# An inverse DFT as half sum and half difference on four row groups of TensorE, with one pool of eight PSUM banks

## Chip, core and metric

The kernel runs on one core of a Trainium2 chip. The metric is the device time in microseconds of one execution. Everything is float32.

## What is computed

The input is x of shape (32, 32, 128, 128): 32 images of 32 channels, each a 128 x 128 matrix. Two residual layers follow each other.

```python
# layer 0: group norm, then 5 Newton-Schulz steps for the matrix square root
for _ in range(NUM_ITER):
    T = 0.5 * (3.0 * I - jnp.matmul(Z, Y))
    Y = jnp.matmul(Y, T)
    Z = jnp.matmul(T, Z)
...
x = x + _L0_conv_ref(_gn(x))
# layer 1: group norm, then a spectral convolution on low modes
x_dht = jnp.fft.fftn(x.astype(jnp.complex64), axes=(2, 3)).real
top = jnp.einsum('bixy,ioxy->boxy', x_dht[:, :, :M1, :M2], weights1)
bot = jnp.einsum('bixy,ioxy->boxy', x_dht[:, :, -M1:, :M2], weights2)
out_dht = out_dht.at[:, :, :M1, :M2].set(top)
out_dht = out_dht.at[:, :, -M1:, :M2].set(bot)
y = jnp.fft.ifftn(out_dht.astype(jnp.complex64), axes=(2, 3)).real
x = x + _L1_conv_ref(_gn(x), weights1, weights2)
```

So of each channel's spectrum 64 row modes (first and last 32) by 32 column modes are kept, mixed over the 32 channels with weights of their own for each mode, and transformed back; only the real part is needed.

## The kernel before, in words

**Newton work.** The 32 images are cut into 256 tasks of four channels each. A task goes through `newton` (with `quartic` twice): ten products (`products`, L250) and three transpositions (`transposed`, L256), each over four 128 x 128 matrices into one PSUM bank, and each followed by an evacuation on DVE (`plus`, L244, with a scalar times PSUM plus a tile) or ACT (`taken`, L236 and L238). Pool makes the operand x (L274) and the sums r (L293, L317), in which `eye` is added. Four tasks run at once in four lanes. One pass of the main loop is a round: every lane makes one step of its generator; a task takes 13 rounds. `prep` computes the group norm of the next image (loads xs, L170; statistics on DVE, L178).

**After a task.** `settle` writes the result to a DRAM buffer mid (L337) and lets Pool make sums and differences of mirrored halves (`fold`, L342); `forward` makes the DFT over one axis, `spectrum` over the other one, with the second group norm, and writes the modes to DRAM (xs<-spec, L449).

**Groups.** The images form three groups of 24, 6 and 2. Once a group's spectra are complete, the queue `prods` gets its mode products (`wide_products` for 24, L492; `small_products` for 6 and for 2, L556), whose results are copied to om by ACT (L499, L569) and written to DRAM (od). The queue `backs` gets one `inverse` for each image of the group, behind a marker that waits for the products.

**Inverse.** `inverse(b)` loads the products twice, on partitions 0 to 63 and 64 to 127 (`load_products`, ob, L589), and the input in pieces of eight channels (`load_input`, yt<-mid, L599, 512 KB each, six buffers). The first stage (L628) transforms the 64 row modes: the channel's products are the stationary operand with 32 columns, and the table (cosines or sines, 128 columns) is streamed. It has 64 matmuls in two blocks, one for each half d. ACT copies the result to gt (L638). The second stage (L646) has, for each d and e, two matmuls with 64 rows and 512 columns, each into a bank. DVE adds the bank to yt in place (L651), and yt is written to the output (`store`, L607), from SP's DMA queue, in the tail from ACT's. In all there are 8 second-stage matmuls and 8 adds of 512 elements per image.

**Banks.** The eight PSUM banks are split: five for the Newton products (`ps_ns`), three for all else (`ps_ax`); only in the tail do the other uses alternate between both.

**Order.** Which instruction comes next on each engine is settled at build time, by a scheduler with priorities from the program order; operations wrapped in `kept` keep their order among themselves. Engines execute their own list in order. The rate at which the queues are stepped is in the main loop:

```python
            if i == 0 or tail:
                step(prods)
            if i == 0 or i == 2 and rounds % 2 or tail:
                step(backs)
```

i is the lane. `tail` holds when no Newton task is left; then both queues are stepped at every lane. At the beginning of the tail the lanes' buffers are freed and the weights for the last products are loaded by 14 DMAs from Pool's queue (wt_late, L746).

Of the kernel before, what the change touches and what calls it, by code (L numbers as in the profile page):

```python
# [24 lines left out]
F32 = mybir.dt.float32  # L25
AF = mybir.ActivationFunctionType
ALU = mybir.AluOpType
AX = mybir.AxisListType
PSUM = bass.MemoryType.PSUM
DRAM = bass.MemoryType.DRAM  # L30

P = 128
B = 32
C = 32
G = 16
LANES = 4
GROUPS = (24, 6, 2)


QA = 3 + 12 ** (1 / 3)  # L40
# [4 lines left out]
NB = 8  # L45
# [7 lines left out]
T_FH = slice(64, 192)  # L53
T_IH = slice(192, 448)
T_IW = slice(448, 576)
T_COLS = 576
# [3 lines left out]
def conv_preact_kernel(  # L60
# [16 lines left out]
    make_identity(nc, ident)  # L77
    eye = const.tile([P, 4, P], F32, name="eye")
    for j in range(4):
        nc.vector.tensor_scalar_mul(eye[:, j, :], ident, EYE)  # L80
    avg_mean = const.tile([P, P], F32, name="avg_mean")
# [27 lines left out]
    sets = phase.enter_context(tc.tile_pool(name="sets", bufs=1))  # L109
    ps_ns = ctx.enter_context(tc.tile_pool(name="ps_ns", bufs=5, space=PSUM))  # L110
    ps_ax = ctx.enter_context(tc.tile_pool(name="ps_ax", bufs=3, space=PSUM))

# [6 lines left out]
    tail = False  # L119
    turn = [0]  # L120

    def bank(pool=None):
        if pool is None:
            pool = ps_ax
            if tail:
                turn[0] += 1
                pool = (ps_ax, ps_ns)[turn[0] % 2]
        return pool.tile([P, 4, P], F32, tag="ps", name="ps")

# [111 lines left out]
    def plus(ps, f, t, tag, bufs=4):  # L241

        s = four(tag, bufs)
        nc.vector.scalar_tensor_tensor(s, ps, f, t, ALU.mult, ALU.add)  # L244
        return s

    def products(lhsT, rhs):
        ps = bank(ps_ns)
        for j in range(4):
            nc.tensor.matmul(ps[:, j, :], lhsT[:, j, :], rhs[:, j, :], start=True, stop=True)  # L250
        return ps

    def transposed(t, pool=None):
        ps = bank(pool)
        for j in range(4):
            nc.tensor.transpose(ps[:, j, :], t[:, j, :], ident)  # L256
        return ps
# [38 lines left out]
    def quartic(m, mb, r):  # L296


        v = plus(products(mb, m), -1 / (QA * QR * QS), m, "v", 3)
        yield  # L300
        w = plus(transposed(v, ps_ns), -QA * QS, r, "w", 3)
        yield
        q = plus(products(v, w), -QA / (16 * QS), eye, "q", 3)
        yield
        return q

    def newton(g, sn, xt, m, mb, r):


        q = yield from quartic(m, mb, r)  # L310
        y = taken(products(q, m), "y")
        yield
        m = taken(products(q, y), "m", 3)
        yield
        mb = taken(transposed(m, ps_ns), "mb", 2, QR * QS)
        r = four("r", 4)
        nc.gpsimd.tensor_tensor(r, mb, eye, ALU.add)  # L317
        yield
        q = yield from quartic(m, mb, r)
        pw, py = products(q, m), products(q, y)  # L320
        w, y = taken(pw, "t", 3), taken(py, "y4", 2)
        yield
        t = plus(products(w, q), -0.5 * EYE / 1.5, eye, "t", 3)
        yield
        ps = products(t, y)
        for j in range(4):
            c = 4 * g + j
            nc.vector.scalar_tensor_tensor(  # L328
                xt[:, j, :], ps[:, j, :], sn[:, c : c + 1], xt[:, j, :], ALU.mult, ALU.add
            )  # L330
        yield
# [17 lines left out]
    def forward(b, q, u):  # L349
# [19 lines left out]
        for i in (1, 0):  # L369
# [5 lines left out]
            )  # L375
        sw = sp.tile([P, 4, P], F32, tag="sw", name="sw", bufs=2)
        nc.scalar.copy(sw, ps)
# [10 lines left out]
    def spectrum(b, u, st):  # L388
# [4 lines left out]
        for s in range(2):  # L393
            for i in range(2):
                for e in range(2):
# [7 lines left out]
                    )  # L403
        z = sp.tile([P, 4, P], F32, tag="z", name="z")
        for i in range(2):
# [29 lines left out]
        ps = transposed(z)  # L435
        spec = sp.tile([P, KK, 4, 8], F32, tag="spec", name=f"spec{b}")
        nc.scalar.activation(
# [18 lines left out]
    def wide_products(i):  # L456
# [26 lines left out]
        for step in range(2 * KK):  # L483
# [3 lines left out]
            if not h:  # L487
                om = modes.tile([P, L * C], F32, tag="om", name=f"om{i}_{kk}", bufs=2)
            pm = bank()
            for t in range(4):  # L490
# [8 lines left out]
            nc.scalar.copy(  # L499
                om.rearrange("p (l t o) -> p t l o", l=4, t=8)[:, 4 * h : 4 * h + 4],  # L500
                pm.rearrange("p t (l o) -> p t l o", l=4),
            )
# [9 lines left out]
    def small_products(i):  # L512
# [35 lines left out]
        for kk in range(KK):  # L548
# [18 lines left out]
            if e:  # L567
                om = modes.tile([P, L * C], F32, tag="om", name=f"om{i}_{k2}", bufs=2)[:, 0:512]
                nc.scalar.copy(om, pm.rearrange("p a x -> p (a x)"))  # L569
                done = k2, om  # L570
                if k2 + len(xks) < KK // 2:
                    load_spectra(k2 + len(xks))
# [6 lines left out]
    def load_products(b):  # L579
        if b < B and b not in obs:  # L580
            g, n = where[b]

            obs[b] = inv.tile([P, 4, 8 * C], F32, tag="ob", name=f"ob{b}", bufs=2)
            if GROUPS[g] <= NB:
                src = od[g][:, :, :, n, :].rearrange("k q l x -> (k q) l x")
            else:
                src = od[g][:, :, n, :].rearrange("k q (l x) -> (k q) l x", l=4)
            for e in range(2):
                kept(nc.sync.dma_start(out=obs[b][64 * e : 64 * e + 64], in_=src))  # L589

    def load_input(b, d):

        if (b, d) in yts:
            return
        yts[b, d] = []
        for e in range(2):
            o = 16 * e + 8 * d
            y = inv.tile([P, 8, P], F32, tag="yt", name=f"yt{b}_{o}", bufs=6)
            kept(nc.sync.dma_start(out=y, in_=mid[b][:, o : o + 8, :]))  # L599
            yts[b, d].append(y)  # L600

    stores = []

    def store(lag):
        while len(stores) > lag:
            b, o, y = stores.pop(0)
            kept((nc.scalar if tail else nc.sync).dma_start(out=out[b, :, o : o + 8, :], in_=y))  # L607

    def inverse(b):

        more = where[b][1] < GROUPS[where[b][0]] - 1
        load_products(b)
        load_input(b, 0)
        yield
        ob = obs[b].rearrange("p l (t o) -> p (l t) o", o=C)
        if more:
            load_products(b + 1)
        for d in range(2):
            store(1)

            pg = [bank() for _ in range(2)]
            for j in range(4):
                for i in range(2):
                    for s in range(2):
                        for e in range(2):
                            col = 64 * i + 32 * s
                            rows = slice(64 * e, 64 * e + 64)
                            nc.tensor.matmul(  # L628
                                pg[e][col : col + 32, j, :],
                                ob[rows, :, 16 * e + 8 * d + 4 * i + j],  # L630
                                tab[rows, T_IH.start + s * P : T_IH.start + (s + 1) * P],
                                start=True,
                                stop=True,
                            )
            gts = []
            for e in range(2):
                gts.append(inv.tile([P, 4, P], F32, tag="gt", name=f"gt{b}_{d}_{e}", bufs=3))
                nc.scalar.copy(gts[e], pg[e])  # L638
            yield
            for e in range(2):  # L640
                store(1)

                py = [bank() for _ in range(2)]
                for i in range(2):
                    rows = slice(64 * i, 64 * i + 64)
                    nc.tensor.matmul(  # L646
                        py[i], tab[rows, T_IW], gts[e][rows], start=True, stop=True
                    )
                for i in range(2):
                    y = yts[b, d][e][:, 4 * i : 4 * i + 4, :]  # L650
                    nc.vector.tensor_add(y, py[i], y)  # L651
                stores.append((b, 16 * e + 8 * d, yts[b, d][e]))
                if not e:
                    if d:
                        if more:
                            load_input(b + 1, 0)
                    else:
                        load_input(b, 1)
                yield
        if not more:  # L660
            store(0)

# [72 lines left out]
    while todo or any(lanes) or posts or specs or prods or backs:  # L735
# [11 lines left out]
        for i in range(LANES):  # L747
# [17 lines left out]
            if i == 0 or tail:  # L765
                step(prods)
            if i == 0 or i == 2 and rounds % 2 or tail:
                step(backs)
# [10 lines left out]
def _table():  # L779
# [11 lines left out]
    t[:, T_FH] = np.tile(half, (2, 1))  # L791
    t[:, T_IH] = np.tile(np.concatenate([np.cos(row).T, np.sin(row).T], 1), (2, 1))
    inv = np.concatenate([np.cos(col).T, -np.sin(col).T], 0) / (P * P)
    t[:, T_IW] = np.tile(inv.reshape(2, 8, 4, P).transpose(0, 2, 1, 3).reshape(64, P), (2, 1))
    return t.astype(np.float32)
# [36 lines left out]
```

## Time and profile before

| what | value |
|---|---|
| time, median of 3 runs | 3305.03 us (3302.87 to 3305.51) |
| the profiled execution | 3304.25 us |
| its span, first to last instruction | 3302.3 us |
| mean granted TensorE clock | 0.986 |
| moved by DMA | 479.64 MB, mean 145 GB/s |
| mode products of the group of 24 | about 2210 to 2400 us |
| last Newton product | 3187.6 us |

The profile is one execution. A line of a group of instructions gives its source line, engine, operation and tiles, the shapes, the count after x, then the busy time in microseconds, the mean of one in nanoseconds, and the idle time of the engine before it with what ended that. A float32 matmul appears as two records on PE (a transposition as one), each with its weight load, so that 256 second-stage matmuls are x512; neighbouring records overlap, and the mean of one is longer than the distance between two. A view by stretches gives, for each stretch of time, the busy time of every engine. The chain of waits follows the last instruction back to what released it.

### The profile page before, as it was taken

What the parts mean: (1) busy time and instruction counts of PE and PEld (TensorE: products, weight loads), DVE (VectorE), ACT (ScalarE), POOL (GpSimd) and SP (SyncE); (2) the same over time, 40 slices, a digit from 0 to 9 for tenths busy, and PEclk for the clock granted to TensorE, in tenths of its full rate; (3) what the DMA queues carried; (4) which work ended last, traced back from release to release, by engine and by line L of the source; (5) the groups of instructions that cost most, each with busy time, mean ns of one, the idle gap of its engine ahead of it and who ended that gap; (6) DMA issues with size and microseconds to landing.
All of it is one profiled execution on the core that took longest, in us unless ns stands there. A gap on an engine that the chain in (4) does not pass through costs nothing.

```text
span 3302.3 us, 82823 instructions
## 1 busy us (share of the span) xinstructions
PE 3180.5 (96%) x33216; PEld 2940.7 (89%) x33216; DVE 2273.3 (69%) x6375; ACT 1388.5 (42%) x2865; POOL 1474.2 (45%) x2077
## 2 busy tenths in 40 slices
PE   6999999999999999999999999999999999999984
PEld 6999999999999999999999999999977777878853
DVE  6777777777777777777777777775566666675551
ACT  3444444444444444444444444444433333433321
POOL 4555555554554545545554555553433333333320
PEclk9999999999999999999999999999999999999996
DMA  3333333333332333333333333326687777777686
GB/s 119 97 103 100 103 100 103 100 98 99 95 93 90 98 102 100 103 100 103 100 97 103 100 100 95 94 91 213 213 260 258 237 231 236 240 255 252 217 286 227
DMA packets 273680, 479.64 MB, mean 145 GB/s; under 512 B 83728, under 2 KB 93968, under 8 KB 273296
## 3 DMA queue, kind: packets, MB, share of 16 engines
q1 hardware_dynamic: 194960, 323.33, 30.9%
q10 hardware_dynamic: 76320, 143.69, 14.1%
q0 software_dynamic: 2016, 7.34, 0.5%
q8 instruction: 261, 4.28, 0.5%
q14 instruction: 123, 1.01, 0.1%
HBM read 319.06 MB, written 155.19 MB: 144 GB/s over the span
## 4 chain that ended last, share of the span: by engine, by line
PE 84%; DMA 8%; DVE 6%; issue 1%; SPq 1%; ACT 0%; DVEq 0%; ACTq 0%
PE ps L250 63%; PE ps L256 11%; DMA xs<-in_xt 5%; PE ps L646 3%; PE ps L628 2%; PE ps L360 1%; DVE xt L328 1%; DVE a_st L178 1%; PE ps L556 1%; PE ps L492 1%; PE ps L397 1%; DMA yt<-mid 1%; DMA out<-yt 1%; DVE q L244 1%; DVE yt L651 1%
## 5 line engine op out<-in xcount | busy, mean ns | idle before, releaser
L342 POOL TENSOR_TENSOR fold<-xt 128x256 f32<-128x256 f32 x512 | 365.2, 732 | 863.6 <-DVE xt L328 762.7
L293 POOL TENSOR_TENSOR r<-b,eye 128x512 f32<-128x512 f32 x256 | 326.5, 1275 | 806.6 <-issue 771.1
L250 PE MATMUL ps<-w,v 128*128 128x128 f32 x4096 | 548.5, 277 | 1.2 <-DVE w L244 1.2
L250 PE MATMUL ps<-y,q 128*128 128x128 f32 x4096 | 543.9, 276 | 0.0
L250 PEld LDWEIGHTS ps<-w,v 128*128 128x128 f32 x4096 | 501.6, 193 | 16.7 <-issue 7.4
L250 PEld LDWEIGHTS ps<-y,q 128*128 128x128 f32 x4096 | 498.8, 192 | 7.7 <-issue 7.6
L236 ACT COPY y<-ps 128x512 f32<-128x512 f32 x512 | 300.3, 587 | 387.8 <-PE ps L250 387.0
L274 POOL TENSOR_SCALAR x<-xt,a_nm,a_sc 128x128 f32<-128x128 f32 x1024 | 449.0, 452 | 21.8 <-DVE a_n L206 20.2
L244 DVE SCALAR_TENSOR_TENSOR w<-ps,r 128x512 f32<-128x512 f32 x512 | 350.0, 686 | 108.8 <-PE ps L256 102.3
L284 ACT ACTIVATE b<-b,a_off,a_scr 128x128 f32<-128x128 f32 x1024 | 422.4, 485 | 1.7 <-DMA b<-in_x 1.6
L244 DVE SCALAR_TENSOR_TENSOR q<-ps,eye 128x512 f32<-128x512 f32 x512 | 349.0, 682 | 56.2 <-PE ps L250 42.0
L178 DVE BATCH_NORM_STATS2 a_st<-xs 128x6 f32<-128x128 f32 x1024 | 228.7, 280 | 189.1 <-DMA xs<-in_xt 188.8
L328 DVE SCALAR_TENSOR_TENSOR xt<-ps,a_t_s,xt 128x128 f32<-128x128 f32 x1024 | 292.4, 342 | 80.5 <-PE ps L250 79.6
L238 ACT ACTIVATE mb<-ps 128x512 f32<-128x512 f32 x256 | 153.0, 598 | 462.5 <-PE ps L256 450.6
L317 POOL TENSOR_TENSOR r<-mb,eye 128x512 f32<-128x512 f32 x256 | 326.0, 1274 | 34.8 <-ACT mb L238 34.5
L256 PE MATMUL ps<-ident,v 128*128 128x128 f32 x2048 | 317.9, 275 | 2.4 <-DVE v L244 2.3
L244 DVE SCALAR_TENSOR_TENSOR v<-ps,m 128x512 f32<-128x512 f32 x256 | 175.7, 686 | 200.9 <-PE ps L250 191.2
L250 PE MATMUL ps<-m,q 128*128 128x128 f32 x2048 | 277.4, 278 | 9.6 <-DVE q L244 9.4
L250 PE MATMUL ps<-x,b 128*128 128x128 f32 x2048 | 276.4, 278 | 5.6 <-POOL x L274 5.6
L250 PE MATMUL ps<-y,t 128*128 128x128 f32 x2048 | 280.3, 280 | 0.4
L236 ACT COPY m<-ps 128x512 f32<-128x512 f32 x256 | 150.0, 586 | 307.7 <-PE ps L250 307.6
L250 PEld LDWEIGHTS ps<-m,q 128*128 128x128 f32 x2048 | 248.9, 192 | 30.2 <-DVE q L244 22.7
(115 smaller groups left out, 5022.8 us busy)
## 6 DMA issues: line engine op xcount, KB each, us to landing
b<-in_x ACTq DMA_DIRECT2D x256, 256.0 KB, 3.0
xt<-in_xt ACTq DMA_DIRECT2D x256, 256.0 KB, 3.3
xs<-in_xt SPq DMA_DIRECT2D x256, 256.0 KB, 3.3
mid<-xt SPq DMA_DIRECT2D x256, 256.0 KB, 2.0
yt<-mid SPq DMA_DIRECT2D x128, 512.0 KB, 6.8
out<-yt SPq DMA_DIRECT2D x110, 512.0 KB, 5.8
ob<-od SPq DMA_DIRECT2D x64, 256.0 KB, 5.3
plain<-in_wk SPq DMA_DIRECT2D x18, 512.0 KB, 4.3
```

The source lines that it names most:

```text
L178: nc.vector.bn_stats(st[:, 4 * i + c, :], tiles[i][:, c, :])
L236: nc.scalar.copy(t, ps)
L238: nc.scalar.mul(t, ps, f)
L244: nc.vector.scalar_tensor_tensor(s, ps, f, t, ALU.mult, ALU.add)
L250: nc.tensor.matmul(ps[:, j, :], lhsT[:, j, :], rhs[:, j, :], start=True, stop=True)
L256: nc.tensor.transpose(ps[:, j, :], t[:, j, :], ident)
L274: nc.gpsimd.tensor_scalar(m[:, j, :], xt[:, j, :], nm[:, c // 2 : c // 2 + 1], sc[:, c : c + 1], ALU.add, ALU.mult,)
L284: nc.scalar.activation(mb[:, j, :], mb[:, j, :], AF.Identity, bias=off[:, c : c + 1], scale=scr[:, c : c + 1],)
L293: nc.gpsimd.tensor_tensor(r, mb, eye, ALU.add)
L317: nc.gpsimd.tensor_tensor(r, mb, eye, ALU.add)
L328: nc.vector.scalar_tensor_tensor(xt[:, j, :], ps[:, j, :], sn[:, c : c + 1], xt[:, j, :], ALU.mult, ALU.add)
L342: nc.gpsimd.tensor_tensor(f[:, :, 64 * half : 64 * half + 64], xt[:, :, 0:64], xt[:, :, 64:128], op)
```

## The change

- The first stage uses the mirror symmetry of the output rows: the table now has the cosines for 64 rows and the sines for 64 rows side by side (128 columns), and the stationary operand is four channels with 32 column modes each (128 columns). It is 8 matmuls with 64 rows for an image instead of 64.
- The second stage treats half an image (16 channels) at once. Each of four row groups of 32 partitions holds four channels. With the cosine table it makes the half sum, with the sine table the half difference, each 4 x 64 columns, into the two halves of a bank; four banks are taken. One row (and its counterpart) goes with the cosine table in a matmul of four columns.
- ACT copies the half differences to a tile d (eight copies of 256 elements per image). DVE adds the half sum to both halves of yt, reading it twice by a broadcast (eight adds of 512 elements, as before). Pool then subtracts and adds d on the two halves of yt, in place (eight operations of 512 elements per image).
- The order of elements in om, od and ob is turned, with the weights reordered on the host; for the groups of 6 and 2 ACT makes a copy of 1024 elements per image (from the tile or to ob).
- `inverse` has five calls instead of eight, and `backs` is stepped at lane 0 in two rounds out of three instead of three times in two rounds; in the tail at every lane, as before. Stores are no longer kept back by one.
- One pool of eight banks serves all. `eye` is one matrix, broadcast over four. sw, z and spec share two buffers; om, d and the first load of the small groups' products share three (`page`).

```diff
-T_IH = slice(192, 448)
-T_IW = slice(448, 576)
+T_IH = slice(192, 320)
+T_IW = slice(320, 576)
...
-    eye = const.tile([P, 4, P], F32, name="eye")
-    for j in range(4):
-        nc.vector.tensor_scalar_mul(eye[:, j, :], ident, EYE)
+    eye1 = const.tile([P, 1, P], F32, name="eye")
+    nc.vector.tensor_scalar_mul(eye1[:, 0, :], ident, EYE)
+    eye = eye1.to_broadcast([P, 4, P])
...
-    ps_ns = ctx.enter_context(tc.tile_pool(name="ps_ns", bufs=5, space=PSUM))
-    ps_ax = ctx.enter_context(tc.tile_pool(name="ps_ax", bufs=3, space=PSUM))
+    ps8 = ctx.enter_context(tc.tile_pool(name="ps8", bufs=8, space=PSUM))
...
+    def page(name):
+        return modes.tile([P, 1024], F32, tag="page", name=name, bufs=3)
+
+    def bank():
+        return ps8.tile([P, 4, P], F32, tag="ps", name="ps")
...
-        sw = sp.tile([P, 4, P], F32, tag="sw", name="sw", bufs=2)
+        sw = sp.tile([P, 4, P], F32, tag="sp", name="sw", bufs=2)
...
             nc.scalar.copy(
-                om.rearrange("p (l t o) -> p t l o", l=4, t=8)[:, 4 * h : 4 * h + 4],
-                pm.rearrange("p t (l o) -> p t l o", l=4),
+                om.rearrange("p (o l) -> p o l", l=L)[:, :, 16 * h : 16 * h + 16],
+                pm.rearrange("p t (l o) -> p o (t l)", l=4),
             )
...
-    def store(lag):
-        while len(stores) > lag:
+    def store():
+        while stores:
...
+        ob = obs[b]
+        if GROUPS[where[b][0]] <= NB:
+            ob = inv.tile([P, 1024], F32, tag="ob", name=f"ob{b}", bufs=2)
+            nc.scalar.copy(
+                ob.rearrange("p (o t l) -> p o t l", t=8, l=4),
+                obs[b].rearrange("p (l t o) -> p o t l", l=4, t=8),
+            )
+        ob = ob.rearrange("p (e j m) -> p e j m", e=2, j=4)
         if more:
             load_products(b + 1)
...
+        pg = [bank() for _ in range(2)]
+        for j in range(4):
             for e in range(2):
-                gts.append(inv.tile([P, 4, P], F32, tag="gt", name=f"gt{b}_{d}_{e}", bufs=3))
-                nc.scalar.copy(gts[e], pg[e])
+                rows = slice(64 * e, 64 * e + 64)
+                nc.tensor.matmul(
+                    pg[e][:, j, :], ob[rows, e, j, :], tab[rows, T_IH], start=True, stop=True
+                )
...
+        for e in range(2):
+            store()
+
+            py = [bank().rearrange("p j x -> p (j x)") for _ in range(4)]
+            py = [p.rearrange("p (s c h) -> p s c h", s=2, h=64) for p in py]
+            cos, sin = (slice(T_IW.start + P * i, T_IW.start + P * i + P) for i in range(2))
+            for s, table, h, g in (
+                (0, cos, slice(0, 64), slice(0, 64)),
+                (1, sin, slice(1, 64), slice(65, 128)),
+                (1, cos, slice(0, 1), slice(64, 65)),
+            ):
+                for i in range(4):
+                    rows = slice(32 * i, 32 * i + 32)
+                    nc.tensor.matmul(
+                        py[i][:, s, :, h],
+                        tab[rows, table],
+                        gts[e][rows, :, g],
+                        start=True,
+                        stop=True,
+                    )
+            d = page(f"d{b}_{e}").rearrange("p (c h) -> p c h", h=64)
+            for i in range(4):
+                nc.scalar.copy(d[:, 4 * i : 4 * i + 4, :], py[i][:, 1])
+            for i in range(4):
+                y = yts[b, e][i // 2][:, 4 * (i % 2) : 4 * (i % 2) + 4, :]
+                y = y.rearrange("p c (s h) -> p c s h", s=2)
+                nc.vector.tensor_tensor(
+                    y, py[i][:, 0, :, None, :].to_broadcast([P, 4, 2, 64]), y, ALU.add
+                )
+            for i in range(2):
+                y, di = yts[b, e][i], d[:, 8 * i : 8 * i + 8, :]
+                for half, op in enumerate((ALU.subtract, ALU.add)):
+                    yh = y[:, :, 64 * half : 64 * half + 64]
+                    nc.gpsimd.tensor_tensor(yh, yh, di, op)
+                stores.append((b, 16 * e + 8 * i, y))
+            if not e:
+                load_input(b, 1)
+            elif more:
+                load_input(b + 1, 0)
             yield
...
-            if i == 0 or i == 2 and rounds % 2 or tail:
+            if i == 0 and rounds % 3 or tail:
                 step(backs)
```

## The prediction

> **What bounds the kernel now.** I read the page's first part, then busy time by stretches, then the groups by tile shape, and last the chain that ended last.
>
> ```profile
> PE 3180.5 (96%) x33216; PEld 2940.7 (89%) x33216; DVE 2273.3 (69%) x6375; ACT 1388.5 (42%) x2865; POOL 1474.2 (45%) x2077
> ```
>
> ```profile
> 1000.00:1500.00 500.00, 497.21 (x4484) 481.68 (x4483) 370.47 (x1070) 225.51 (x472) 255.09 (x360) 1.00 0.32 97
> ...
> 2400.00:3188.00 788.00, 769.33 (x9750) 626.32 (x9750) 508.26 (x1275) 296.66 (x600) 258.52 (x362) 0.98 0.75 243
> 3188.00:3303.00 115.00, 54.43 (x1629) 35.88 (x1610) 25.03 (x55) 16.56 (x31) 14.23 (x19) 0.70 0.73 258
> ...
> 3190.00:3200.00 10.00, 6.78 (x156) 3.46 (x152) 3.85 (x7) 1.67 (x3) 3.69 (x3) 1.00 1.00 329
> 3200.00:3210.00 10.00, 7.87 (x82) 3.82 (x84) 4.09 (x7) 2.80 (x6) 6.21 (x10) 0.66 0.99 333
> ```
>
> The columns of a stretch are length, busy us of PE, PE's weight loads, DVE, ACT and Pool, granted clock, DMA share, GB/s. There are three regimes. Up to about 2400 us TensorE is the bound (497 of 500 us) and DMA is a third used. From 2400 to 3188 the Newton work shares PE with the inverse transforms: PE is idle 18.7 us of 788 and DMA is at 0.75. After the last Newton product at 3188 comes a tail of 115 us in which PE is half idle and DMA full: 329 to 333 GB/s at a share of 1.00 is the ceiling that I use for it.
>
> ```profile
> L646 PE MATMUL ps<-gt,tab 64*128 64x512 f32 x512 | 156.5, 658 | 19.4 <-ACT gt L638 10.0 <-DVE yt L651 9.4
> L628 PE MATMUL ps<-tab,ob 64*32 64x128 f32 x4096 | 86.7, 291 | 10.6 <-DMA ob<-od 6.7 <-DVE yt L651 3.7
> ...
> L651 DVE TENSOR_TENSOR yt<-ps,yt 128x512 f32<-128x512 f32 x256 | 166.7, 684 | 125.4 <-PE ps L646 108.0 <-DMA yt<-mid 15.7 <-PE ps L150 1.0
> ...
> L317 POOL TENSOR_TENSOR r<-mb,eye 128x512 f32<-128x512 f32 x256 | 326.0, 1274 | 34.8 <-ACT mb L238 34.5
> ...
> L406 ACT COPY z<-ps 128x256 f32<-128x256 f32 x64 | 20.7, 375 | 85.8 <-PE ps L397 81.1 <-DVE b_d L154 4.7
> ```
>
> These price the pieces: the two PE stages of the inverse, the add on DVE, a 512-element two-input Pool operation (1274 ns) and a 256-element ACT copy out of PSUM (375 ns). The last pieces of the chain:
>
> ```profile
> 3218.96 14.23 DMA xs<-spec
> ...
> 3234.51 3.65 DMA diag<-xs
> ...
> 3238.36 2.41 PE ps L556 x133
> ...
> 3266.72 0.59 ACT om L569
> ...
> 3280.63 6.66 DMA out<-yt
> ...
> 3287.37 9.63 DMA yt<-mid x2
> ```
>
> The last group's mode products cannot begin before its spectrum has been written and read back (3219 to 3238); they take 28.3 us, and the last two inverses another 35.6 us, up to 3302.3.
>
> **What the Trainium skill says.** "TensorEngine Tiling (Array Packing)", Key Properties: tiles operate independently, and a change of tiling mode drains the array. The trace agrees: the four records of an L646 block, each 512 columns or 0.43 us at the Newton rate of 0.107 us per 128 columns, take 1.06 us and not 1.7, and the block costs about 0.1 us on entering. "TensorE: Matmul & The Clock Gate", Why this matters for your kernels: four K=32 tiles with N=512 gave 3.07 times one; no run here shows four row tiles yet. "SBUF — State Buffer", SBUF: two separate sides: Pool and DVE exclude each other where DVE reads two SBUF inputs; the adds here read one from PSUM, and L651 ran at 684 ns beside a Pool that is 33% busy, so I charge nothing.
>
> **The change, part by part.**
>
> *PE per image.* Before: first stage 64 matmuls in two blocks; in the timeline a block runs 2695.94 to 2697.09 with 0.15 us of switching, 1.3 us; second stage four blocks of 1.06 us plus 0.09 of switching. 2 x 1.3 + 4 x 1.15 = 7.2 us. After: the first stage is 8 matmuls of 128 columns, four on each of two row groups; a 128-column matmul is two records 0.107 to 0.111 us apart, so 4 x 0.22 = 0.88, with switching 1.1 us. The second stage, for each half image, is 256 + 252 + 4 columns on each of four row groups. At two records of 0.213, two of 0.21 and two short ones bounded by their weight load (0.11, the spacing of two loads on the same rows) this is 1.07 us if the groups run side by side, 1.3 with switching; 4.3 if they do not. I take 1.3: 1.1 + 2 x 1.3 = 3.7 us. Saved: 3.5 us an image.
>
> *Where the images stand.* A step of the inverse was taken 1.5 times a round and an image took 8 calls, 5.3 rounds; now it is taken in two rounds of three and needs 5 calls, 7.5 rounds. In the instruction order of PE 28 of the 32 inverses stand before the last Newton matmul; in the changed kernel only 21 do. Seven images move into the tail.
>
> *End of the Newton work.* 3187.6 - 28 x 7.2 + 21 x 3.7 = 3063.7. To this come stalls. Of the 18.7 us idle before I keep all. New: DVE now gets four adds in a row (4 x 0.684 = 2.7 us) while PE has 1.3 us of its own; before two adds (1.4) met 1.15. Each of the adds also waits for ACT's copy of the same bank, and four of the eight banks are held meanwhile. 42 half images at nothing (as the slack of a round covers it) to 1.0 us; I take 0.15, 6 us: 3070. Pool gets 8 x 1.274 = 10.2 us an image. Its old work in an image's time is 258.5 us / 28 images, x 7.5/5.3 = 13 us; 23 us of the (3070 - 2400) / 21 = 32 us of an image are busy. Behind these operations stands r for the next w; it has two rounds (6 us) of slack, so I charge nothing, and 1 us per half (42 us) if that cover is gone.
>
> *Tail up to the last products.* The instruction order has images 21 to 29 after the Newton end, and the write of the last spectrum is queued on SP behind the loads of image 29, which wait for the stores of image 28. So eight images must pass. An image moves 2.1 MB in, 2.1 out and 0.5 of products: 4.7 MB at 330 GB/s is 14.3 us. Pool's own chain for an image is 10.2, plus for each half the second store's issue (0.34, on ACT's queue, ahead of the next copies), and two copies (0.75) with hand-overs of 0.2: 12.8 us, below DMA. 8 x 14.3 = 114; the late weights (14 x 512 KB, 7.3 MB, at the 411 GB/s of 3220 to 3230) 18; six buffers already filled, 3.1 MB, -9: 123 us. The spectrum's write and read back took 19 us under load; the queue is emptier now, 3.4 and 3.7 are medians: I take 10 (7 to 19). Products begin at 3070 + 133 = 3203, against 3238.
>
> *End.* 28.3 for the products as before, to 3231. From the last om copy to the end 35.6 before; added are a copy of 1024 elements on ACT (1.1 to 2.4, twice the 512-element rows at 0.59 and 1.2) and Pool's chain, four halves of 6.4 us behind 13 us of loads and first stage, and a store of 4.5: 43. Span 3231.5 + 0.3 + 43 = 3275.
>
> *At nothing.* One pool of eight banks: PE's order to 2200 us is the same but for a few swaps per image, and PE idles 0.5% there, so nothing to gain; a bank taken at a bad moment could cost up to 0.3% of 2200, 7 us. The broadcast eye, shared sw/z/spec buffers and the other strides of om: same element counts on engines with over a quarter of idle time; u's copy (375 ns for 256 with a stride of 512 bytes in PSUM) shows that the stride costs nothing.
>
> The profiled execution lasted 3304.25, 1.95 more than its span, and the median is 3305.03. 3275 + 2 = 3277 us, 0.8% less.
>
> **Rivals.**
> 1. *The tail is paced by Pool and ACT's queue (slower).* A store on ACT waits for Pool, and the next copies, for which Pool waits, stand behind it; Pool also issues the late weights and waited 15.4 us for them before. For it: DVE, Pool, ACT, store and load follow one another in only six buffers. Against: in 3190 to 3213 two images passed in 24 us with the same buffers. From 7.15 to 8.55 us a half image (20 halves at 1.4 = 28 us) the gain is gone; at 9.3 the time is 3320. Chance 0.22.
> 2. *The Newton stretch stalls* on DVE's or Pool's runs, 0.6 us more per half image: 42 x 0.6 = 25, 3302, no change. For it: Pool goes from a third to over 70% busy in this stretch. Against: each Newton round now meets fewer adds on DVE, 8 in 7.5 rounds instead of 8 in 5.3. 0.16.
> 3. *Better than forecast*: 12.3 us per image, as the last two before, and half of the old stalls gone: 16 + 9 less, and the end 8 less: 3244. 0.12.
> 4. *The row groups do not run side by side*: 42 x 3.0 = 126 us later, about 3400. L646 at two groups speaks against it. 0.04.
>
> **How the numbers follow.** The forecast has 0.46, with a range of its own of 3255 to 3297. What tells from no change is 0.2%, 6.6 us, so 3298 to 3312. Rival 2 is mostly there (0.13, the rest slower). Faster 0.46 + 0.12 = 0.58, same 0.13, slower 0.22 + 0.04 + 0.03 = 0.29. The range 3240 to 3328 leaves out rival 4, a third of rival 1 and small ends of the others.
>
> **What would show it.** Second-stage matmuls starting in fours a few ns apart, blocks near 1.1 us; the last Newton product near 3070; a DMA share near 1.00 from there for some 120 us with halves every 7 us; the first product of the last group near 3203; 43 us after its last copy. Wrong it would be if the Newton end came after 3095, or if DMA sat under 0.8 in the tail with Pool waiting for ACT, or if PE before 2200 us lost more than 1%.

## The result and the profile after

The changed kernel takes 3400.37 us (median, 3399.22 to 3405.13) against 3305.27 us for the kernel before beside it: a ratio of 1.0286, interval 1.0267 to 1.0306. It is slower by 2.9%; the forecast was 3277 us. Its profiled span is 3403.3 us (3302.3 before), so the question is where 101 us came from, and 129 us against the span of 3275 us that the prediction worked out.

The first part of the page of the changed kernel:

```profile
PE 3108.6 (91%) x30656; PEld 2973.8 (87%) x30656; DVE 2320.0 (68%) x6372; ACT 1448.5 (43%) x3065; POOL 1787.0 (53%) x2333
```

TensorE did 72 us less than before, as intended, and stood idle 295 us instead of 122. The view by stretches of the changed kernel (length; busy us of PE, its weight loads, DVE, ACT, Pool; granted clock, DMA share, GB/s) shows where:

```profile
500.00:1000.00 500.00, 491.49 (x4428) 475.88 (x4427) 368.07 (x1047) 224.54 (x467) 252.55 (x358) 1.00 0.31 96
...
2450.00:3000.00 550.00, 492.46 (x4653) 463.12 (x4652) 387.58 (x976) 238.24 (x540) 362.74 (x422) 0.96 0.63 206
...
3265.00:3280.00 15.00, 7.38 (x68) 6.89 (x68) 7.09 (x16) 5.45 (x12) 10.10 (x9) 0.50 0.97 322
...
3350.00:3403.00 53.00, 14.15 (x149) 12.01 (x148) 9.94 (x16) 11.17 (x23) 19.72 (x16) 0.50 0.59 184
```

and the same second stretch of the kernel before:

```profile
2450.00:3000.00 550.00, 535.03 (x6215) 433.32 (x6221) 372.23 (x958) 211.03 (x431) 189.18 (x268) 0.98 0.73 239
```

Three things are to be seen. In the first regime, where no inverse runs, PE now idles 8.5 us of 500 instead of 2.7 (497.34 busy before). In the second it idles 57.5 us of 550 instead of 15, while Pool goes from 189 to 363 us busy. In the tail DMA is near its ceiling at 3265, and far from it in the last 53 us.

The groups by shape of the changed kernel, for the instructions that are new:

```profile
L652 PE MATMUL ps<-gt,tab 32*128 32x256 f32 x512 | 59.6, 509 | 54.0 <-ACT gt L636 48.5 <-DVE yt L665 5.4
...
L665 DVE TENSOR_TENSOR yt<-ps,yt 128x512 f32<-128x512 f32 x256 | 158.9, 682 | 194.7 <-ACT d L661 88.5 <-DMA yt<-mid 55.4 <-POOL yt L672 41.1
...
L661 ACT COPY d<-ps 128x256 f32<-128x256 f32 x256 | 76.9, 385 | 145.2 <-POOL yt L672 61.1 <-PE ps L652 53.5 <-DMA yt<-mid 12.2
...
L672 POOL TENSOR_TENSOR yt<-yt,d 128x512 f32<-128x512 f32 x256 | 317.6, 1273 | 187.6 <-DVE yt L665 140.4 <-issue 41.9 <-DMA plain<-in_wk 5.2
```

Their durations are those of the forecast (682 and 684, 1273 and 1274 ns). What is new stands behind the bar: the copy L661 waits for Pool, Pool for the add L665, the add for the copy.

To find the place of each loss I use three points of the trace in every kernel: A, the start of the first Newton record after four fifths of them (16384 of 20480); the last Newton product; and the end. The stretch lies between the first two and contains the inverses that share PE; the tail follows it. These points are good to about 0.2 us.

| kernel | A | stretch | last Newton product | tail | of it: to the last group's products, they, after them | span |
|---|---|---|---|---|---|---|
| before | 2338.8 | 848.4 | 3187.2 | 115 | 51, 28, 36 | 3302.3 |
| after | 2379.2 | 791.1 | 3170.4 | 233 | 150, 30, 53 | 3403.3 |
| forecast | as before | 118 less | 3070 | 204 | 133, 28, 43 | 3275 |

A comes 40 us late, the stretch saved 57 us and not 118, and the tail is 28 us longer than forecast. The sum is 40 + 61 + 28 = 129.

### The profile page after: what moved, and what is told of

The parts are those of the page before. It is cut to its first block, busy times and chain, and to the rows that moved or that the text cites. A ratio compares the mean times of both kernels' runs of the same rounds, so it can differ in the third digit from the quotient of the medians.

```text
span 3403.3 us, 78408 instructions
## 1 busy us (share of the span) xinstructions
PE 3108.6 (91%) x30656; PEld 2973.8 (87%) x30656; DVE 2320.0 (68%) x6372; ACT 1448.5 (43%) x3065; POOL 1787.0 (53%) x2333
## 5 line engine op out<-in xcount | busy, mean ns | idle before, releaser
L289 POOL TENSOR_TENSOR r<-b,eye 128x512 f32<-128x512 f32 x256 | 326.2, 1274 | 646.2 <-issue 600.0
L672 POOL TENSOR_TENSOR yt<-yt,d 128x512 f32<-128x512 f32 x256 | 317.6, 1273 | 187.6 <-DVE yt L665 140.4
L665 DVE TENSOR_TENSOR yt<-ps,yt 128x512 f32<-128x512 f32 x256 | 158.9, 682 | 194.7 <-ACT d L661 88.5
```

What stands on the lines that cost most here:

```text
L672: nc.gpsimd.tensor_tensor(yh, yh, di, op)
```

## The experiments

Eleven kernels, each timed beside the kernel before. A, stretch, tail and span are from one profile each; median and ratio (to the kernel before) are from all runs. Runs of one kernel differ by up to 20 us (a_yield: 3329.62 to 3349.43), and A of a_nopool lies 5 us behind that of the changed kernel, though its edit acts only behind A. So a difference of some 10 us between two stretches proves little by itself.

| kernel | edit | A | stretch | tail | span | median | ratio, interval |
|---|---|---|---|---|---|---|---|
| b_pool8 | before, one bank pool | 2377.6 | 846.3 | 115 | 3338.5 | 3343.31 | 1.0111, 1.0094 to 1.0128 |
| a_yield | after, a step more in prep | 2331.2 | 780.5 | 230 | 3341.9 | 3337.57 | 1.0094, 1.0065 to 1.0123 |
| a_nopool | after, no L672 | 2384.4 | 759.6 | 208 | 3352.1 | 3350.10 | 1.0121, 1.0101 to 1.0140 |
| a_pace | after, old stepping | 2378.1 | 885.5 | 114 | 3377.7 | 3383.43 | 1.0230, 1.0214 to 1.0246 |
| b_pool8_yield | b_pool8 and the step | 2329.5 | 839.0 | 115 | 3283.6 | 3283.81 | 0.9928, 0.9914 to 0.9941 |
| a_yield_xsact | a_yield, xs from ACT | 2324.2 | 760.7 | 230 | 3315.1 | 3321.15 | 1.0037, 1.0022 to 1.0051 |
| a_yield_halfadds | a_yield, half the adds | 2333.8 | 757.9 | 234 | 3325.9 | 3319.63 | 1.0035, 1.0023 to 1.0048 |
| a_yield_spstore | a_yield, tail stores from SP | 2333.9 | 774.1 | 245 | 3353.5 | 3355.92 | 1.0135, 1.0120 to 1.0150 |
| a_free3 | a_nopool, a_yield_xsact, a_yield_halfadds | 2324.4 | 711.8 | 207 | 3242.8 | 3243.90 | 0.9807, 0.9794 to 0.9821 |
| b_pool8_yield_xsact | b_pool8_yield, xs from ACT | 2320.4 | 846.2 | 115 | 3281.4 | 3283.47 | 0.9924, 0.9910 to 0.9937 |
| a_xsact_pace | a_yield_xsact, old stepping | 2323.7 | 880.3 | 116 | 3320.2 | 3318.80 | 1.0034, 1.0021 to 1.0047 |

**The 40 us before any inverse.** Of the change, the bank pool, the shared buffers and the broadcast eye act there (and, near its end, the order of om). The waits of PE in 500 to 1000 us of the changed kernel begin with a line that the kernel before doesn't have (total us, times, longest):

```profile
PE ps L184 <- DVE a_qs L180: 7.1, 5, 1.4
```

Five images pass in that stretch, and each pays once. At one of these places the timeline of PE in the changed kernel (start, us) has

```profile
1033.28 0.26 PE L146 MATMUL ps<-a_ms,avg_mean 128*128 128x16 f32 x1
1034.97 0.38 PE L184 MATMUL ps<-a_qs,avg_mean 128*128 128x32 f32 x2 [1.43 <-DVE a_qs L180]
```

and that of DVE

```profile
1033.58 0.17 DVE L148 COPY a_nm<-ps 128x16 f32<-128x16 f32 x1 [0.26 <-PE ps L146]
1033.79 0.24 DVE L150 TENSOR_TENSOR a_d<-a_st,a_nm 128x64 f32<-128x64 f32 x1
1034.06 0.23 DVE L153 TENSOR_TENSOR a_d<-a_d 128x64 f32<-128x64 f32 x1
1034.32 0.25 DVE L154 SCALAR_TENSOR_TENSOR a_d<-a_d,a_st 128x64 f32<-128x64 f32 x1
1034.60 0.22 DVE L180 TENSOR_REDUCE a_qs<-a_d 128x32 f32<-128x64 f32 x1
```

The matmul for the mean of the group norm (L146) and the one for its mean square (L184) stand next to each other on PE, and between them lies a chain of five DVE instructions: PE has nothing else in its list and waits, 1.7 us between the two records where neighbours are 0.11 apart. In the instruction list of the kernel before Newton products stand between the two in 30 of 32 images; in the changed kernel in none. About 1.6 us (1.69 less 0.11) for each of the 25 images up to A is 40.

b_pool8 puts only the pool into the kernel before:

```diff
-    ps_ns = ctx.enter_context(tc.tile_pool(name="ps_ns", bufs=5, space=PSUM))
-    ps_ax = ctx.enter_context(tc.tile_pool(name="ps_ax", bufs=3, space=PSUM))
+    ps8 = ctx.enter_context(tc.tile_pool(name="ps8", bufs=8, space=PSUM))
+    ps_ns = ps_ax = ps8
```

> The kernel before with one edit: one pool of eight PSUM banks in place of five and three. In the instruction order of this kernel all 32 pairs of small matmuls of the group norm (mean, then mean square) stand next to each other on PE, as in the changed kernel; with five and three there are Newton matmuls between them in 30 of 32. Theory A (PE, in order, waits at the second matmul for a chain on DVE, about 1.6 us an image): about 33 us are lost by the 15360th Newton record and the time is 3335 to 3350 us. Rival (the loss before 2200 us comes from the broadcast eye or the shared small buffers, the bank pool costs nothing): under 8 us lost there, 3300 to 3312.

A came at 2377.6, 38.8 us late, with nothing of the new inverse in the kernel, the time of 3343.31 lies in the range of theory A, and its waits of PE in 500 to 1000 us begin with the same line, under its own numbers:

```profile
PE ps L188 <- DVE a_qs L184: 7.1, 5, 1.4
```

a_yield leaves the pool and only parts the two matmuls, by one step more of the generator:

```diff
         _, nm, d = moments(st, "a")
+        yield
         q = small.tile([P, C], F32, tag="a_qs", name=f"a_qs{b}")
```

> The changed kernel with one more step boundary in the group norm between the mean and the mean-square matmul, so that Newton matmuls stand between the two again (31 of 32). Theory A: the 33 us up to the 15360th Newton record come back, and some more later; 3355 to 3368 us. Rival (the DVE chain or the other shared buffers cost the time and not the neighbouring of the two matmuls): 3390 to 3403.

A came at 2331.2, 48 us earlier than in the changed kernel and 7.6 earlier than before; the stretch lost another 10.6. The time of 3337.57 is below the range expected, 3355 to 3368, as A comes even earlier than in the kernel before. So the pool costs 40 us by the order that it brings about, and not by a lack of banks. With both edits in the kernel before (b_pool8_yield: the two diffs above)

> The kernel before with one pool of eight banks and the step boundary between the two small matmuls of the group norm. In its order 16 Newton matmuls stand between them in 31 images. The changed kernel with the boundary was 12 us ahead of the kernel before at the 15360th Newton record. If that gain belongs to the bank pool and the boundary alone: 12 us ahead there as well, the rest as before, 3288 to 3296. Rival (the gain came with another part of the change, the broadcast eye or the shared buffers): level with before, 3300 to 3310.

PE is busier than in either kernel; the first regime in b_pool8_yield:

```profile
500.00:1000.00 500.00, 497.89 (x4510) 483.97 (x4509) 372.05 (x1077) 228.86 (x475) 255.31 (x364) 1.00 0.34 101
1000.00:1500.00 500.00, 498.84 (x4522) 485.28 (x4522) 372.70 (x1076) 229.59 (x476) 256.53 (x364) 1.00 0.32 96
```

This version beats both kernels; it is 0.7% under the kernel before. Whether the step alone, with five and three banks, would do as well was not tried.

b_pool8_yield and a_yield differ by the new inverse alone, with its stepping, its buffers and the broadcast eye: A agrees within 2 us, the stretch gains 58.5, the tail loses 115. The rest of the experiments divides these two numbers.

**The stretch: 61 us of the saving missing.** The blocks themselves are cheap. The second stage of a half image in the timeline of PE:

```profile
2714.91 1.06 PE L246 MATMUL ps<-w,v 128*128 128x128 f32 x8
2715.89 1.26 PE L652 MATMUL ps<-gt,tab 32*128 32x256 f32 x24
2717.08 1.16 PE L246 MATMUL ps<-m,q 128*128 128x128 f32 x8
```

From its start to the next product it is 1.19 us. The Newton block ahead of it takes 0.98 where 0.89 is usual, so 0.09 us are lost on entering: together 1.28, where 1.3 was forecast. A first stage takes 1.09 and 0.09, 1.18 in all (1.1). By the forecast's terms 21 x 3.7 are 78 us, the other work of the stretch is 628 (848.4 - 28 x 7.2 - 18.7), and the old idle time 18.7: together 724, and 791 were measured. 67 us are new stalls, where 6 were charged. PE's idle time in the stretch shows most of them: 80 us, and 19 in the kernel before.

The longest waits of PE in 2450 to 3000 us of the changed kernel are all for DVE:

```profile
PE ps L252 <- DVE v L240: 18.0, 9, 4.7
PE ps L184 <- DVE a_qs L180: 11.4, 4, 6.0
PE ps L246 <- DVE t L240: 11.3, 4, 7.6
PE ps L246 <- DVE q L240: 7.5, 8, 1.9
```

One such place in the timeline of the changed kernel:

```profile
2717.57 2.48 DVE L665 TENSOR_TENSOR yt<-ps,yt 128x512 f32<-128x512 f32 x4 [0.88 <-ACT d L661]
...
2718.94 4.95 POOL L672 TENSOR_TENSOR yt<-yt,d 128x512 f32<-128x512 f32 x4 [1.83 <-DVE yt L665]
...
2720.89 0.63 DVE L150 TENSOR_TENSOR b_d<-b_st,b_nm 128x64 f32<-128x64 f32 x1
...
2721.56 1.19 DVE L153 TENSOR_TENSOR b_d<-b_d 128x64 f32<-128x64 f32 x1
...
2722.79 1.21 DVE L154 SCALAR_TENSOR_TENSOR b_d<-b_d,b_st 128x64 f32<-128x64 f32 x1
...
2724.17 0.68 DVE L240 SCALAR_TENSOR_TENSOR v<-ps,x 128x512 f32<-128x512 f32 x1
...
2725.16 0.35 PE L417 MATMUL ps<-avg_v,b_qr 128*128 128x1 f32 x2 [2.23 <-DVE b_qr L413]
```

Three group-norm operations that take 0.24 us elsewhere take 0.63, 1.19 and 1.21 while Pool's four run, each ending about 0.1 us after one of Pool's does. What follows them on DVE, a v and then b_qr (L413), is late, and PE idles 2.2 us for b_qr.

a_nopool takes Pool's four away; the half differences are then not added (the sine part is missing):

```diff
-                for half, op in enumerate((ALU.subtract, ALU.add)):
-                    yh = y[:, :, 64 * half : 64 * half + 64]
-                    nc.gpsimd.tensor_tensor(yh, yh, di, op)
```

> The changed kernel without Pool's half-difference operations (left out: the subtraction and addition of the sine part, so the output lacks it). Theory B (Pool's 4.9 us runs hold up DVE's two-operand operations in the Newton stretch and, with ACT's store issues, pace the tail at 7.3 us a half image): the stretch from the 16384th to the 20480th Newton record falls from 791 to about 755 us, the tail after the last Newton product from 233 to about 195; 3325 us. Rival C (loads of the statistics input and DMA set both): stretch 785 or more, tail 225 or more, 3385 or more. Between them, each part is read by its own stretch.

The stretch is 31.5 us shorter and the tail 25, close to theory B for the first (755 expected, 759.6 measured) and short of it for the second (195, 208); the time of 3350 is above its 3325. The groups of DVE by shape, in 2440 to 3150 us only, of the changed kernel

```profile
L150 DVE TENSOR_TENSOR b_d<-b_st,b_nm 128x64 f32<-128x64 f32 x6 | 8.2, 1372 | 0.1
L154 DVE SCALAR_TENSOR_TENSOR b_d<-b_d,b_st 128x64 f32<-128x64 f32 x6 | 3.4, 568 | 0.2
L153 DVE TENSOR_TENSOR b_d<-b_d 128x64 f32<-128x64 f32 x6 | 3.3, 548 | 0.2
```

and of a_nopool

```profile
L154 DVE SCALAR_TENSOR_TENSOR b_d<-b_d,b_st 128x64 f32<-128x64 f32 x6 | 1.5, 248 | 0.2
L150 DVE TENSOR_TENSOR b_d<-b_st,b_nm 128x64 f32<-128x64 f32 x6 | 1.5, 242 | 0.1
L153 DVE TENSOR_TENSOR b_d<-b_d 128x64 f32<-128x64 f32 x6 | 1.3, 225 | 0.2
```

show what is held up: 1372 ns against 242. The six behind this mean differ widely. Two take 2.87 and 3.46 us, as older operations of Pool follow L672 without a gap; the longest, and Pool beside it:

```profile
3102.20 3.46 DVE L150 TENSOR_TENSOR b_d<-b_st,b_nm 128x64 f32<-128x64 f32 x1
...
3100.45 2.53 POOL L672 TENSOR_TENSOR yt<-yt,d 128x512 f32<-128x512 f32 x2
3102.90 1.44 POOL L338 TENSOR_TENSOR fold<-xt 128x256 f32<-128x256 f32 x2
3104.27 1.30 POOL L313 TENSOR_TENSOR r<-mb,eye 128x512 f32<-128x512 f32 x1
```

With the same three operations of the other norm, DVE was held some 13 us longer (21.9 us in all against 8.8), which is less than half of the 31.5; the rest goes with what waits behind Pool itself (its other operations, and the stores on SP), and wasn't divided further.

a_yield_halfadds asks what the run of four adds costs. It leaves out half of the cosine part:

```diff
                 y = y.rearrange("p c (s h) -> p c s h", s=2)
+                if i % 2:
+                    continue
                 nc.vector.tensor_tensor(
```

> The changed kernel with the boundary and with two of the four adds of every half image left out (half of the channels lack the cosine part): DVE's run is 1.4 us instead of 2.7, its length before the change. Theory E (the run of four adds and the wait of each for ACT's copy hold up the Newton evacuations, 1 us a half image): the stretch falls from 780 to about 740. Rival C (late loads of xs): 772 or more.

757.9 against 780.5 in a_yield: 22.6 us, for 1.24 us less of DVE in each of 42 half images (52 us). Theory E, with 40, had about twice as much.

a_yield_xsact moves the loads of the next image's statistics from SP's queue to ACT's:

```diff
-            kept(nc.sync.dma_start(out=t, in_=xt_in[b, :, 4 * i : 4 * i + 4, :]))
+            kept(nc.scalar.dma_start(out=t, in_=xt_in[b, :, 4 * i : 4 * i + 4, :]))
```

> The changed kernel with the boundary, and with the loads of the statistics input (xs) issued from ACT's queue and not from SP's, where they stand behind stores that wait for Pool. Theory C (DVE stands in order behind these late loads, 48 us of waits between 2450 and 3000 us, and PE with its shorter inverse has nothing to cover it): the stretch falls from 780 to 745 to 760, and the total by as much, to about 3310. Rival (the loads are late because the DMA engines are busy, not because they are issued late, or DVE's runs of adds set the pace): stretch 775 or more.

19.8 us less in the stretch, at the edge of what theory C expected, and A comes 7 us earlier. The medians fell by less than the two together, 16 us. The reason for trying it was this wait of DVE in 2450 to 3000 us of the changed kernel, with SP's stores before those loads waiting for Pool:

```profile
DVE a_st L174 <- DMA xs<-in_xt: 46.8, 19, 8.4
```

But the kernel before has it too, and as long:

```profile
DVE a_st L178 <- DMA xs<-in_xt: 45.9, 20, 7.1
```

It can hardly have cost more there than PE's idle time, 15 us of the 550. If it cost little because PE had 7.2 us of its own work in each image, the same edit should be worth little in b_pool8_yield:

> The kernel before with one bank pool, the boundary, and xs issued from ACT's queue. In the kernel before PE idles 18.7 us in the Newton stretch, and DVE waits 46 us for xs there, which PE's longer inverse mostly covers. If so, early xs are worth little here: stretch 839 falls to 830 to 836, total 3275 to 3283. Rival (xs costs the same as in the changed kernel, 20 us): stretch under 822, total 3268 or less.

It was worth nothing: A came 9 us earlier, the stretch went from 839.0 to 846.2, the ratio from 0.9928 to 0.9924. But this doesn't settle why. The same wait in 2450 to 3000 us of b_pool8_yield and b_pool8_yield_xsact

```profile
DVE a_st L178 <- DMA xs<-in_xt: 48.4, 22, 8.7
DVE a_st L178 <- DMA xs<-in_xt: 45.8, 16, 9.1
```

and of a_yield and a_yield_xsact

```profile
DVE a_st L174 <- DMA xs<-in_xt: 48.3, 18, 8.6
DVE a_st L174 <- DMA xs<-in_xt: 30.5, 14, 5.6
```

show that the edit hardly shortened the wait in the first pair, and by 18 us in the second. That the wait did not grow is shown; that it costs more because its cover on PE went is the likely reading, and is not shown.

a_free3 has the edits of a_nopool, a_yield_halfadds and a_yield_xsact at once, and its output lacks what those of the first two lack.

> The changed kernel with the boundary, xs issued from ACT's queue, Pool's half-difference operations left out and two of four adds of every half image left out (the output lacks the sine part and half of the cosine part). If Pool's runs, DVE's runs of adds and the late xs loads together are what eats PE's saving in the Newton stretch, it must come out near PE's own sum: 848 - 28 x 7.2 + 21 x 3.7 = 724 us, so 720 to 735. Rival (another limit, such as the four banks held at once, remains): 745 or more. Tail about 205 as without Pool's work; total 3265 to 3285.

The stretch takes 711.8 us, 68.7 less than in a_yield, near the sum of the three alone (31.5 + 22.6 + 19.8 = 74), and below the 724 of PE's own work and old idle time. In 2450 to 3000 us PE of a_free3 is busy

```profile
2450.00:3000.00 550.00, 527.56 (x6027) 501.10 (x6027) 355.93 (x961) 260.21 (x591) 222.56 (x315) 0.99 0.73 240
```

so these three, with the step, are as much as the new stalls, and the rival of another limit (745 us or more) is out. That it falls below 724, and below the 720 to 735 expected, has a second part: for the same number of records in its stretch PE is busy 686 us, and 711 in the changed kernel, at a mean granted clock of 0.99 instead of 0.96. So the stalls appear not only as idle time but also as slower work. That idle time brought the lower clock was not tested.

**Where the images stand.** a_pace goes back to three steps in two rounds:

```diff
-            if i == 0 and rounds % 3 or tail:
+            if i == 0 or i == 2 and rounds % 2 or tail:
```

> The changed kernel with the old stepping of the inverse queue (three steps in two rounds), so that by the instruction order 30 instead of 22 first stages stand before the last Newton matmul. If an image in the Newton stretch costs PE's 3.7 us and the stalls seen (about 60 us for 21 images, 2.9 each), 8 images move from 15 us each in the tail to 6.6 each: about 3335. Rival (with the images closer together, DVE, Pool and DMA set the pace and an image costs as much there as in the tail): 3390 to 3410.

The tail is 114 us, that of the kernel before, and the stretch 885.5, 94.4 more. By the trace 30 first and 30 second stages now stand in it, and 22 and 21 in the changed kernel: eight to nine images, where PE's share of them is some 32 us. The exchange gains 26 us of span and 17 of the median; the 3383 measured are far from the 3335 expected and near the rival's 3390. a_xsact_pace repeats it with a_yield_xsact as its base:

> The changed kernel with the boundary, xs from ACT's queue and the old stepping of the inverse queue. The old stepping alone gave 17 us, as 8 images cost 11.8 us each in the Newton stretch instead of 15 in the tail. If early xs lower that cost, more is won: 3285 to 3300. Rival (Pool and DVE are full when images come closer together, so the gains do not add): 3305 to 3325.

880.3 and 116: the stretch and the tail trade 120 against 114, so nothing is gained once the order and the loads are mended, as its rival had it. Divided by eight to nine, one inverse more costs 13 to 15 us in the tail, and 10 to 15 in the stretch when they stand this close there.

**The tail: 28 us more.** The end of the changed kernel, from the timeline of Pool, of ACT and of DVE:

```profile
3379.92 4.94 POOL L672 TENSOR_TENSOR yt<-yt,d 128x512 f32<-128x512 f32 x4 [2.35 <-issue]
3387.21 4.92 POOL L672 TENSOR_TENSOR yt<-yt,d 128x512 f32<-128x512 f32 x4 [2.35 <-issue]
```

```profile
3382.44 2.79 ACTq L606 DMA_DIRECT2D out<-yt  x2
3385.32 1.20 ACT L661 COPY d<-ps 128x256 f32<-128x256 f32 x4 [5.11 <-POOL yt L672]
```

```profile
3385.78 2.48 DVE L665 TENSOR_TENSOR yt<-ps,yt 128x512 f32<-128x512 f32 x4 [4.80 <-POOL yt L672]
```

Pool ends a half image at 3384.86. Only then is the second store issued on ACT's queue; the copies of the next half stand behind it and begin at 3385.32, the adds at 3385.78, and after two of them Pool goes on at 3387.21. The period is 7.29 us, of which Pool works 4.94. Further up in the tail, with loads beside it, a whole image takes 15.0 us (first stages at 3239.1, 3254.4, 3269.0, 3283.6, 3298.9), a little over two such periods, at a DMA share of 0.94 to 1.03: there both limits are near at once. In a_nopool the way to the products takes 138 us instead of 150 and the end 39 instead of 53, so 25 us of the tail go with Pool's operations. That is not quite the missing 28: the forecast's 43 us for the end had a part of Pool's chain in them.

a_yield_spstore takes the stores off ACT's queue:

```diff
-            kept((nc.scalar if tail else nc.sync).dma_start(out=out[b, :, o : o + 8, :], in_=y))
+            kept(nc.sync.dma_start(out=out[b, :, o : o + 8, :], in_=y))
```

> The changed kernel with the boundary, and with the stores of the tail issued from SP's queue in place of ACT's, so that ACT's copies no longer stand behind a store that waits for Pool. Theory D (the tail's half image takes 7.3 us as Pool's 4.9 + store issue 0.4 + copy 0.4 + two adds 1.4 follow one another): the last four half images come 5.2 apart, the end part falls by 6 us and the tail from 230 to about 215. Rival (SP's loads, now behind the stores, come later, and DMA paces the tail at 14.6 us an image): tail 228 or more.

The end of Pool's timeline in this run:

```profile
3326.34 9.84 POOL L673 TENSOR_TENSOR yt<-yt,d 128x512 f32<-128x512 f32 x8 [59.68 <-DVE yt L666]
3339.74 9.92 POOL L673 TENSOR_TENSOR yt<-yt,d 128x512 f32<-128x512 f32 x8 [3.56 <-DMA out<-yt]
```

The loop is broken: two half images now follow each other on Pool without a gap (theory D expected 5.2 us from one to the next, it is 4.9). But the second image waits for its loads, which on SP follow the stores of the first; Pool pauses 3.56 us there. The end went only from 51 to 48 us, and the way to the products from 149 to 167, where SP stands 74 us for Pool ahead of its stores. The rival was right too: the tail as a whole became 15 us longer.

## Why the prediction was wrong

**At nothing, the pool of banks.** This step failed first: it called the change of order before 2200 us "a few swaps per image" and bounded it at 7 us. The swaps put two matmuls side by side of which one waits for a chain that starts from the other, in every image. 40 us at A, shown by b_pool8 (38.8) and by its going away in a_yield. The other edits of that part cost nothing that can be seen: b_pool8, without them, has the same A as the changed kernel within 2 us.

**End of the Newton work, the charge for stalls.** PE's cost per image was right (1.28 and 1.18 against 1.3 and 1.1), and so was the number of images moved. (Newton records are 0.112 us apart in the trace, and not 0.107; little hangs on it.) The term 42 x 0.15 = 6 us measured 67. Three parts of it were charged at nothing or near it: Pool's runs, judged only by the r behind them (31.5); four adds in a row (22.6); the late loads of the statistics, not in the sum at all (19.8); 10.6 more are the same swapped pair, whose wait was up to 6 us here. They add to 85, more than 67; that the edits overlap in part and take old idle time too is a guess, and the noise of single profiles is in each. The prediction expected Pool's rise from a third to over 70% (363 of 550 us, 66%, were measured), but looked only at what Pool feeds.

**The SBUF lock.** The Trainium skill, "SBUF — State Buffer", SBUF: two separate sides, says that a DVE operation with two SBUF inputs and a Pool operation that reads SBUF exclude each other, the later one blocking until the first is done. The prediction checked the new adds, which have one input in PSUM, and charged nothing. They indeed kept their 682 ns. But the lock falls on any DVE operation of that kind that comes by, and the group norms have three each: 1372 ns against 242 agrees with what the page states. In one point it is more than that sentence says: the 3.46 us operation was not let in between four operations of Pool in a row.

**Tail.** The DMA term was right: in a_nopool an image takes 14.5 us (first stages from 3205.7 to 3263.7 in four steps), and 14.3 were forecast. Pool's chain was put at 6.4 us a half image and measured 7.29: the sum had the issue of a store and two copies, and left out the two adds (1.3 us) that Pool waits for in between. At 7.15 for DMA the forecast took the larger of two close numbers; the loss is 17 us before the products (12 of them go with Pool's operations, 138 us in a_nopool; the rest was not divided), 2 in them, and 10 at the end (53 against 43), where no DMA covers the chain.

**The rivals.** Rival 4 is refuted by the 1.28 us; that its figure, about 3400, is the time measured is chance. Rivals 1 and 2 both happened, 1 with 25 us instead of the 28 or more that it needed, 2 with 67 instead of 25. They had been written as cases that exclude each other, and the range took one at a time; the misses of 40, 61 and 28 us add up. Of the signs named for being wrong, the Newton end after 3095 (3170) and the loss of more than 1% before 2200 us (8.5 of 500 us idle, 2.7 before) came. The third, DMA under 0.8 with Pool waiting for ACT, came only in the last 53 us (0.59).

## What to carry to other kernels

When a pool of PSUM banks is changed, compare the built order of PE for pairs of instructions that are joined through another engine and have come to stand next to each other: one step between them was worth 48 us at A here. An engine whose work per step is halved may uncover what others did meanwhile: price the waits that cost little before (46 us of late loads) anew. Work given to Pool is charged to whom Pool holds up, not only to whom it feeds, and a queue that carries a store and the copies behind it is added up all round the loop.

## What the runs showed of the hardware

- Four row groups of 32 partitions worked side by side: 24 records of 256, 252 and 4 columns, a quarter on each group, the four of a set 6 to 7 ns apart, in 1.19 us and 0.09 on entering, near the 1.07 estimated for one group alone. The Trainium skill, "TensorE: Matmul & The Clock Gate", Why this matters for your kernels, has 3.07 for four such tiles; here it is about 3.4, the 4.3 us estimated for the four in a row by the 1.28 measured.
- In the tail, with the granted clock at 0.50, the records of a first stage took 2.08 us instead of 1.16, from the first start to the last end. What this cost was not measured; PE was busy 14 of the last 53 us.
- A DVE operation of 64 elements with two SBUF inputs, 242 ns in a_nopool, took 1372 ns on the mean and 3.46 us at most beside Pool's operations. The adds with one input in PSUM stayed at 682 ns.
